# Sixteen graphs on one core: the last graph's head sums added in the bank, its last head finished apart, the check in steps, three casts on VectorE

## The chip, the cores and the metric

The kernel runs on one core of a Trainium2 chip. The metric is the device time of one execution, in microseconds (us); less is better. The engines are TensorE (PE; its loads of weights are shown on a row of their own, PEld), VectorE (DVE), ScalarE (ACT), GpSimd (POOL) and SyncE (SP), which issues the transfers here. Each engine runs its own instructions in order and waits for the others by semaphores.

## The reference, cut to what matters

Sixteen graphs of 1024 nodes with 256 features. Two layers, each followed by a layer norm over a residual sum:

```python
# layer 0: gated sum over neighbours; adj is 0 or 1 in these inputs, symmetric, with ones on the diagonal
e = leaky(einsum('bid,bjd->bij', h * a[:, 0], h))      # leaky: slope 0.2
alpha = sigmoid(where(adj == 1, e, -max))              # kinds 2 to 4 likewise with a1 to a3
x = layernorm(x + einsum('bij,bjd->bid', alpha, h) + bias)
# layer 1: graph attention, 4 heads of 64 features
Wh = (X @ W).reshape(B, N, H, F)
e = leaky_relu(e_src[:, :, None, :] + e_dst[:, None, :, :], 0.2)
alpha = softmax(where(A > 0, e, -1e9), axis=2)
x = layernorm(x + elu(einsum('bijh,bjhf->bihf', alpha, Wh)))
```

The kernel doesn't form the softmax of layer 1 edge by edge. exp(leaky_relu(s + d)) is one product of an exponential of s and one of d where s + d is positive, and another such product where it is negative. So for each head it sums two sets of columns over the neighbours j: 64 features times one factor and 64 times the other, with the two factors themselves (2 x 64 + 2 = 130 columns, called E) over the *positive* edges, and the second set (66 columns, F1) over *all* edges; the negative edges are the difference.

## The kernel before, in words

A graph has NB = 8 blocks of P = 128 nodes, in NH = 2 halves of 4 blocks (NQ = 4); a half has two pairs of blocks. `stages()` makes, for each graph, some fifty generators, one for each stage; a step of a stage issues one or a few instructions. `issue()` sorts all steps of all graphs by due times and issues them in that order: a table of times for each stage, FIRST for graph 0, TIMES for graphs 1 to 14, LAST for graph 15, with 112 added per graph. These times only order the instructions on each engine; when they run is set by the queues and semaphores. In the body, one graph's layer 0 overlaps the layer 1 of the graph before. All this stands in a block where the order is taken as written. What touches the change, with line numbers:

**The adjacency.** A block of it, 128x1024 int32, is loaded into one of two buffers (a32; aload), cast to bf16 on ScalarE (a16, one buffer; L273), with the sum of each row taken on the way (`sums`), turned (L283 on TensorE for graph 0, into a PSUM bank; L288 by a transposing DMA for the others), and written as a mask of bytes mT by ScalarE (L295, with the row sums of the squares). The two row sums are compared at the end.

**Layer 0.** The scores e (L344), leaky relu (L356 ACT, L364 DVE), sigmoid (L370 ACT), transpositions of the gate (L383 PE) and its products with the mask (L389 and L400 DVE, L407), the aggregation agg (L415 PE, 128x128 by 128x256), the residual, and the norm's parts: statistics (L432 and L438 DVE), rstd (L456 and L457, GpSimd), shift (L465 DVE), norm (L477 ACT, L475 DVE for some).

**Layer 1.** yT and the projection (L486 to L517), the two factors for each head (`product` L602 or L607), and gm, the matrix that the sums multiply. gm is held as two fp32r parts, a high one (L621 ACT) and the rest (L628 DVE), side by side: for each head and block of j, 130 high columns and then 130 low ones. `pos` (L646 DVE) writes the positive edges of a head and a half, 128x512 for each block j, into one of six buffers, from the sources broadcast by a DMA (sbc, L636 SP). The sums over the positive edges are `acc` (L658 PE): for each half and head, 8 blocks j by 4 blocks of targets q, lhsT a 128x128 piece of pos, rhs the 260 columns of gm (high and low at once), accumulated over j into a PSUM bank for each q; two PSUM tiles of two banks hold a head, and there are two such tiles (ps_u), so a head must be read out of them before the next head's sums begin. Each head is read out by a copy of its low part by ScalarE (L673) and an addition of high and low by VectorE (L681) into the tile u. The sums over all edges, tot (L701 PE), use the mask as fp32r (allm, L693 ACT) and 264 columns of gm, the high and the low part by two matmuls into the same columns: 

```python
for l in range(2):
    nc.tensor.matmul(tot[:, 0 : H * F1], lhsT=t["allm", ib, jb // 4 * 4][:, jb % 4, :],
        rhs=pl.gm[:, :, jb, l, F:E], ...
```

**The end of a graph.** For a pair of blocks and all four heads at once: total_kept or total_less (L728 ACT, L734 DVE), `weigh` (L746 ACT for the last two graphs, L758 DVE else: the second set, total less positive, times rho), `divide` (L768 to L773: sum of the sets, the softmax's denominator, its reciprocal rz, the product), `elu` (L793 ACT), `join` (L785 and L787 DVE), then the norm's parts again and `leave` (L802 SP, the store; L804 DVE, a running maximum of rz over the graphs, zinv).

**The check.** After the ordered block (L1316 to L1337) VectorE and TensorE work out whether the shortcuts held: the difference of the row sums (each entry 0 or 1), the span of the exponents, and the greatest rz, reduced and compared, transposed to one partition and reduced to a flag. `values_load` (L1339) brings the flag to the engines, and a branch (L1342) does all graphs again in a general way if it is set. With these inputs it isn't taken.

Of the kernel before, what the change touches and what calls it, by code (L numbers as in the profile page):

```python
# [8 lines left out]
F32 = mybir.dt.float32  # L9
# [160 lines left out]

class FastPools:
# [25 lines left out]
def stages(nc, k, pl, b, xg, adjg, outg, sums, span, zinv):  # L197
# [71 lines left out]
    def cast():  # L269
        for ib in range(NB):  # L270
            t["a16", ib] = pl.adjp.tile([P, N], BF16, tag="a16", name="a16", bufs=1)
            at = b * NB + ib
            nc.scalar.activation(  # L273
                t["a16", ib], t["a32", ib], AF.Copy, accum_out=sums[:, 0, at : at + 1]
            )
            yield
# [374 lines left out]

    def acc():
        for half, h in HEADS:
            for pair in range(NQ // 2):
                t["acc", half, h, pair] = pl.ps_u.tile([P, 2, HALF], F32, tag="u", name="acc")
            for jb in range(NB):
                for q in range(NQ):
                    nc.tensor.matmul(  # L658
                        t["acc", half, h, q // 2][:, q % 2, 0 : 2 * E],
                        lhsT=t["pos", half, h, jb][:, q * P : (q + 1) * P],  # L660
                        rhs=pl.gm[:, h, jb].rearrange("p l f -> p (l f)"),
                        start=(jb == 0),
                        stop=(jb == NB - 1),
                    )
                yield

    def acc_low():
        for half, h in HEADS:
            for pair in range(NQ // 2):
                low = t["low", half, h, pair] = pl.work.tile(  # L670
                    [P, 2, E], F32, tag="low", name="low", bufs=2
                )
                nc.scalar.copy(low, t["acc", half, h, pair][:, :, E : 2 * E])  # L673
                yield

    def acc_sum():
        for half, h in HEADS:
            for pair in range(NQ // 2):
                if h == 0:
                    t["u", half, pair] = pl.us.tile([P, 2, H, E], F32, tag="us", name="u")  # L680
                nc.vector.tensor_tensor(  # L681
                    t["u", half, pair][:, :, h, :],
                    t["acc", half, h, pair][:, :, 0:E],
                    t["low", half, h, pair], ALU.add,
                )
                yield
# [27 lines left out]
    def parts(half, pair):  # L714

        u = t["u", half, pair]
        return u[..., 0:F], u[..., F : 2 * F], u[..., 2 * F], u[..., 2 * F + 1]

    def second(half, pair):

        return t["u", half, pair][..., F : 2 * F + 1]

# [18 lines left out]
    def times(val, by):  # L741

        if late:
            for q in range(2):
                for h in range(H):
# [7 lines left out]
    def weigh():  # L753
        for half, pair in PAIRS:
            ib = half * NQ + 2 * pair
            u2 = second(half, pair)
            if half:
                nc.vector.tensor_tensor(u2, t["ts", pair][..., 0 : F + 1], u2, ALU.subtract)  # L758
                yield
            times(u2, t["rho"][:, ib : ib + 2])  # L760
            yield

    def divide():
        t["rz"] = small("rzs", NB, H)
        for half, pair in PAIRS:
            ib = half * NQ + 2 * pair
            o, u2, z2, z1 = parts(half, pair)
            nc.vector.tensor_tensor(o, o, u2, ALU.add)  # L768
            yield
            rz = t["rz"][:, ib : ib + 2]  # L770
# [8 lines left out]
    def join():  # L779
        for half, pair in PAIRS:  # L780
            o, ex, _, _ = parts(half, pair)
            yp = t["y", half][:, 2 * pair : 2 * pair + 2, :].rearrange(
                "p q (h f) -> p q h f", h=H
            )
            nc.vector.scalar_tensor_tensor(o, o, 0.0, yp, ALU.max, ALU.add)  # L785
            yield
            nc.vector.scalar_tensor_tensor(yp, ex, 1.0, o, ALU.min, ALU.add)  # L787
            yield

    def elu():  # L790
        for half, pair in PAIRS:
            o, ex, _, _ = parts(half, pair)
            nc.scalar.activation(ex, o, AF.Exp)  # L793
            yield

    def leave():
        for half in range(NH):
# [5 lines left out]
            if half == NH - 1:  # L803
                nc.vector.tensor_tensor(zinv, zinv, t["rz"], ALU.max)  # L804
            yield

# [11 lines left out]
        weigh=weigh(), divide=divide(), elu=elu(), join=join(),  # L818
        moments1=moments("1"), gathered1=gathered("1"),
        spread1=spread("1"), shift1=shift("1"), norm1=norm("1"), leave=leave(),  # L820
    )

# [104 lines left out]
    "leave": [206.44, 240.93],  # L927
}
FIRST = {
    "aload": [-145.70, -145.40, -144.40, -143.60, -141.20, -140.10],  # L930
    "cast": [-146.10, -145.60, -144.60, -143.90, -142.60, -142.00, -140.90, -139.50],
    "turn": [-145.90, -145.10, -144.50, -143.20, -142.30, -141.30, -140.30, -139.30],
    "mask": [-145.30, -144.90, -143.80, -142.80, -141.70, -141.10, -139.40, -139.10],
    "setup": [-142.90, -140.70, -138.30],
    "xt": [-147.20, -147.10, -147.00, -146.80],
    "xtc": [-146.90, -146.70, -146.60, -146.40],
    "xta": [-146.50, -145.80, -144.20, -142.20, -141.80, -139.90, -139.60, -137.00],
    "score": [
        -146.20, -145.50, -144.80, -144.70, -143.40, -143.10, -142.10, -141.50, -140.40,
        -138.90, -138.60, -136.60,  # L940
    ],
    "leak": [
        -145.20, -144.30, -144.10, -144.00, -143.00, -142.70, -141.60, -141.40, -139.70,
        -138.50, -137.70, -136.40,
    ],
    "leaky": [
        -145.00, -143.70, -143.50, -143.30, -142.40, -141.90, -141.00, -140.60, -139.20,
        -137.90, -137.30, -135.60,
    ],
    "sigmoid": [-142.50, -140.80, -138.20, -137.10, -136.10, -135.00, -133.50, -132.80],  # L950
    "below": [
        -140.50, -140.20, -138.80, -138.00, -137.50, -136.80, -135.70, -135.20, -134.30,
        -132.70,
    ],
    "lower": [
        -140.00, -139.80, -138.40, -136.70, -136.00, -135.90, -134.90, -134.70, -133.40,
        -131.90,
    ],
    "upper": [-139.00, -137.60, -136.50, -135.10, -134.20, -133.00, -132.30, -131.80],
    "self_loop": [-138.70, -137.40, -135.50, -134.60, -133.80, -132.50, -131.60, -131.20],  # L960
    "agg": [
        -138.10, -137.80, -137.20, -136.20, -135.30, -134.80, -134.50, -133.90, -133.60,
        -133.20, -132.60, -132.40, -132.10, -131.40, -131.30, -130.60,
    ],
    "residual": [-136.90, -134.40, -133.70, -133.30, -133.10, -132.00, -130.90, -130.20],
    "moments0": [-135.80, -134.10, -132.90, -132.20, -131.10, -130.70, -130.40, -130.10],
    "gathered0": [-135.40, -134.00, -131.70, -131.50, -130.50, -130.30, -96.07, 17.17],
    "spread0": [-131.00, 20.28],
    "shift0": [-130.80, 24.26],
    "norm0": [6.67, 11.00, 11.41, 12.51, 25.36, 25.99, 26.71, 27.01],  # L970
    "yt": [17.15, 19.47, 29.04, 29.13],
    "ytc": [19.36, 19.69, 29.17, 29.53],
    "project": [20.27, 22.38, 25.24, 26.22, 32.78, 40.85, 41.12, 41.80],
    "wh": [25.15, 27.94, 28.22, 36.80, 41.06, 42.84, 42.85, 44.25],
    "sources": [43.57, 44.67],
    "rows": [44.50, 47.17],
    "keep_rows": [46.30, 54.62],
    "top_dve": [46.04, 47.34, 49.10, 49.48, 50.03],
    "top_pe": [46.11, 49.26],
    "exps": [51.13],  # L980
    "product": [51.24, 51.61, 51.65, 55.99, 64.09, 71.97, 73.66, 74.28],
    "high": [54.44, 56.34, 58.73, 61.00, 69.95, 72.79, 74.04, 74.66],
    "low": [54.68, 57.50, 65.30, 66.50, 71.75, 77.68, 77.72, 77.72],
    "sload": [50.22, 76.32, 79.88, 84.60, 99.79, 115.99, 126.87, 141.84],
    "pos": [
        56.38, 56.65, 59.61, 60.83, 61.90, 62.47, 66.98, 72.25, 78.79, 79.58, 80.30,
        81.29, 81.91, 83.89, 85.64, 86.24, 94.25, 94.83, 97.97, 99.15, 100.99, 101.36,
        101.95, 101.97, 105.63, 106.23, 106.73, 107.47, 108.82, 109.31, 109.42, 109.44,
        111.05, 111.90, 112.37, 114.78, 114.79, 114.81, 115.82, 117.22, 117.23, 120.53,
        122.14, 122.30, 123.00, 123.69, 124.94, 127.40, 128.22, 130.84, 132.75, 133.15,  # L990
        134.26, 137.15, 140.15, 141.06, 143.44, 144.05, 145.63, 146.94, 153.65, 154.27,
        155.46, 159.89,
    ],
    "acc": [
        61.10, 61.65, 61.72, 63.59, 69.81, 72.90, 74.47, 75.10, 81.40, 83.30, 83.92,
        84.50, 84.62, 86.15, 88.72, 89.34, 98.53, 98.69, 100.90, 100.97, 102.11, 102.79,
        105.80, 106.18, 108.03, 108.18, 108.25, 109.02, 109.72, 109.72, 110.35, 110.44,
        113.56, 114.38, 116.31, 117.04, 117.43, 119.10, 119.20, 119.89, 122.26, 122.73,
        122.79, 124.03, 124.41, 124.82, 125.15, 127.73, 134.85, 139.77, 140.29, 142.76,
        143.64, 145.00, 145.14, 146.56, 153.78, 155.85, 158.96, 159.35, 164.01, 166.21,  # L1000
        166.25, 166.99,
    ],
    "acc_low": [
        76.14, 76.54, 89.55, 94.31, 106.18, 107.05, 110.80, 113.01, 119.96, 120.50,
        133.26, 133.40, 149.44, 150.74, 167.23, 167.69,
# [382 lines left out]
```

## Time and profile before

| | us |
|---|---|
| median of 3 runs | 1748.97 (1747.94 to 1749.34) |
| the profiled execution's own time | 1748.92 |
| its span, first to last instruction | 1747.1 |
| PE (TensorE) busy | 1695.6 (97%), mean granted clock 0.990 |
| DVE (VectorE) busy | 1639.0 (94%) |
| ACT (ScalarE) busy | 1237.6 (71%) |
| POOL (GpSimd) busy | 107.1 (6%) |
| acc: 4096 matmuls 128x260, L658 | 613.3, 293 ns for one |
| u<-acc,low: 256 additions, L681 | 102.1, 419 ns for one |
| low<-acc: 256 copies, L673 | 89.9, 377 ns for one |
| a<-a: 128 casts, L273 | 135.6, 1060 ns for one |

Busy time is the sum of an engine's instructions, as a share of the span. The duration of a matmul is not its cost: matmuls are pipelined, and the distance from one to the next is shorter than either. "Idle before" is the time for which an engine stood still just ahead of a group's instructions, with the event that ended it. The granted clock is the TensorE clock as a share of full speed. A row of a timeline is a run of like instructions: its start, its length, engine, line, operation, tiles, shape and number, and in brackets the wait ahead of it.

### The profile page before, as it was taken

The numbers are of one execution on the slowest core, as the hardware profiler recorded it, in microseconds if no ns is written. First come the engines' busy times: TensorE is split into PE (matmuls) and PEld (weight loads), VectorE is DVE, ScalarE is ACT, GpSimd is POOL, SyncE is SP. The second block draws the span as 40 slices with busy tenths as digits, with TensorE's granted clock in tenths as the row PEclk, the third lists the DMA queues.
The fourth block names the chain that finished last, engine by engine and source line by source line (L and its number), as shares of the span: only waits on it lengthen the run. The fifth ranks groups of instructions, "written<-read, shape, count | busy, mean of one in ns | idle before, by whom it ended". The sixth has DMA issues, their size and how long they took to land.

```text
span 1747.1 us, 29629 instructions
## 1 busy us (share of the span) xinstructions
PE 1695.6 (97%) x10579; PEld 1494.8 (86%) x10579; DVE 1639.0 (94%) x3640; ACT 1237.6 (71%) x2770; POOL 107.1 (6%) x138
## 2 busy tenths in 40 slices
PE   7999999999999999999999999999999999999884
PEld 4789898998979889898998989889898998979883
DVE  4498999999999999999999999999999999999997
ACT  6673967759587685967759586685957769585675
POOL 0001000010000101000010000101000010000100
PEclk9999999999999999999999999999999999999987
DMA  5452343434334343343434334343342435331020
GB/s 184 109 127 75 93 109 88 109 91 129 90 90 101 109 119 91 98 98 91 109 93 135 81 98 108 99 115 91 97 110 78 109 74 139 79 74 49 26 67 26
DMA packets 249274, 168.60 MB, mean 97 GB/s; under 512 B 133280, under 2 KB 232736, under 8 KB 249120
## 3 DMA queue, kind: packets, MB, share of 16 engines
q1 hardware_dynamic: 249120, 166.63, 36.3%
q8 instruction: 86, 1.41, 0.3%
q14 instruction: 68, 0.56, 0.1%
HBM read 118.10 MB, written 17.04 MB: 77 GB/s over the span
## 4 chain that ended last, share of the span: by engine, by line
PE 83%; issue 7%; DVE 4%; ACT 3%; DMA 1%; POOL 0%; SPq 0%; POOLq 0%; ACTq 0%; DVEq 0%
PE agg L415 24%; PE acc L658 24%; PE tot L701 13%; PE e L344 11%; PE pw L505 6%; PE pg L383 2%; DVE pos L646 1%; PE pt L308 1%; PE pt L486 1%; DMA sbc<-sdram 1%; DMA aT<-a 0%; ACT mT L295 0%; ACT a L273 0%; DVE gm L628 0%; DVE gate L364 0%
## 5 line engine op out<-in xcount | busy, mean ns | idle before, releaser
L646 DVE SCALAR_TENSOR_TENSOR pos<-sbc,nd,mT 128x512 fp32r<-128x512 f32 x1024 | 732.0, 738 | 7.6 <-DMA sbc<-sdram 4.5
L658 PE MATMUL acc<-gm,pos 128*128 128x260 f32 x4096 | 613.3, 293 | 6.5 <-DVE u L681 2.8
L658 PEld LDWEIGHTS acc<-gm,pos 128*128 128x128 f32 x4096 | 538.7, 190 | 19.5 <-issue 3.8
L415 PE MATMUL agg<-xb,gate 128*128 128x256 f32 x2048 | 463.3, 379 | 0.0
L415 PEld LDWEIGHTS agg<-xb,gate 128*128 128x128 f32 x2048 | 380.0, 190 | 46.9 <-DVE gate L407 0.6
L701 PE MATMUL tot<-gm,allm 128*128 128x264 f32 x2048 | 328.4, 297 | 7.1 <-ACT gm L621 5.0
L701 PEld LDWEIGHTS tot<-gm,allm 128*128 128x128 f32 x2048 | 281.1, 190 | 11.7 <-ACT gm L621 5.2
L344 PE MATMUL e<-xT,xTa 128*128 128x512 f32 (+3 forms) x768 | 265.6, 490 | 3.1 <-ACT xTa L332 1.6
L344 PEld LDWEIGHTS e<-xT,xTa 128*128 128x128 f32 x768 | 135.3, 191 | 106.9 <-issue 53.4
L673 ACT COPY low<-acc 128x260 f32<-128x260 f32 x256 | 89.9, 377 | 190.3 <-PE acc L658 190.3
L693 ACT CAST allm<-mT 128x512 fp32r<-128x512 uint8 x256 | 157.5, 616 | 27.9 <-PE tot L701 26.6
L477 ACT ACTIVATE y<-y,shift,rstd 128x256 f32<-128x256 f32 x254 | 136.8, 591 | 41.8 <-DVE shift L465 41.8
L273 ACT ACTIVATE a<-a 128x1024 bf16<-128x1024 int32 x128 | 135.6, 1060 | 41.0 <-DMA aT<-a 19.3
L295 ACT ACTIVATE mT<-aT 128x1024 uint8<-128x1024 bf16 x120 | 127.2, 1060 | 6.4 <-DMA aT<-a 6.3
L456 POOL TENSOR_SCALAR std<-mv 128x4 f32<-128x4 f32 x64 | 27.0, 421 | 1626.0 <-DVE mv L438 1426.5
L364 DVE TENSOR_TENSOR gate<-e,gate 128x512 f32<-128x512 f32 x192 | 104.2, 550 | 21.3 <-ACT gate L356 21.2
L505 PE MATMUL pw<-w_aug,yT 128*128 128x264 f32 x512 | 122.2, 387 | 0.7 <-ACT yT L495 0.6
L681 DVE TENSOR_TENSOR u<-acc,low 128x260 f32<-128x260 f32 x256 | 102.1, 419 | 16.6 <-ACT low L673 16.6
L432 DVE BATCH_NORM_STATS2 st<-y 128x6 f32<-128x256 f32 x256 | 105.8, 415 | 1.2
L505 PEld LDWEIGHTS pw<-w_aug,yT 128*128 128x128 f32 x512 | 93.4, 190 | 15.6 <-ACT yT L495 1.7
L356 ACT ACTIVATE gate<-e 128x512 f32<-128x512 f32 x192 | 90.0, 486 | 14.6 <-PE e L344 14.5
L400 DVE TENSOR_TENSOR gate<-gate,mT 128x1024 f32<-128x1024 f32 (+7 forms) x128 | 95.8, 748 | 4.5 <-PE pg L383 2.4
(97 smaller groups left out, 1775.9 us busy)
## 6 DMA issues: line engine op xcount, KB each, us to landing
a<-in_adj_dram SPq DMA_DIRECT2D x128, 512.0 KB, 4.7
sbc<-sdram SPq DMA_DIRECT2D x128, 256.0 KB, 4.6
out_dram<-y SPq DMA_DIRECT2D x31, 512.0 KB, 3.5
xb<-in_x_dram SPq DMA_DIRECT2D x15, 1024.0 KB, 5.2
aT<-a SPq DMA_TRANSPOSE x120, 3.1
xb<-in_x_dram SPq DMA_DIRECT2D x2, 512.0 KB, 4.2
sdram<-srow SPq DMA_DIRECT2D x32, 8.0 KB, 1.4
out_dram<-y SPq DMA_DIRECT2D x2, 256.0 KB, 2.3
```

What stands on the lines that cost most here:

```text
L273: nc.scalar.activation(t["a16", ib], t["a32", ib], AF.Copy, accum_out=sums[:, 0, at : at + 1])
L295: nc.scalar.activation(t["mT"][:, :, ib * P : (ib + 1) * P], t["aT", ib], AF.Square, accum_out=sums[:, 1, at : at + 1],)
L344: nc.tensor.matmul(e[:, 0:n], lhsT=t["xTa", jb][:, c, :], rhs=t["xT"][:, c, at : at + n], start=(c == 0), stop=(c == DC - 1),)
L364: nc.vector.tensor_tensor(ge, t["e", jb, at][:, 0:n], ge, ALU.max)
L415: nc.tensor.matmul(agg[:, 0:D], lhsT=t["gate"][:, jb, ib * P : (ib + 1) * P], rhs=t["xb"][:, jb, :], start=(jb == 0), stop=(jb == NB - 1),)
L432: nc.vector.bn_stats(st, t["y", half][:, q, :])
L477: nc.scalar.activation(y, y, AF.Identity, bias=shift, scale=rstd)
L505: nc.tensor.matmul(pw[:, 0:WD], lhsT=t["yT"][:, c, jb * P : (jb + 1) * P], rhs=k.w_aug[:, c, :], start=(c == 0), stop=(c == DC - 1),)
L646: nc.vector.scalar_tensor_tensor(p_, t["sbc", half, h], t["nd"][:, jb, h : h + 1], t["mT"][:, jb, half * HALF : (half + 1) * HALF], ALU.is ...
L658: nc.tensor.matmul(t["acc", half, h, q // 2][:, q % 2, 0 : 2 * E], lhsT=t["pos", half, h, jb][:, q * P : (q + 1) * P], rhs=pl.gm[:, h, jb] ...
L693: nc.scalar.copy(m_, t["mT"][:, j0 : j0 + 4, ib * P : (ib + 1) * P])
L701: nc.tensor.matmul(tot[:, 0 : H * F1], lhsT=t["allm", ib, jb // 4 * 4][:, jb % 4, :], rhs=pl.gm[:, :, jb, l, F:E], start=(jb == 0 and l == 0),
```

## The change

It has five parts.

1. In the last graph (`whole`), an acc step issues two matmuls of 130 columns, high and low, with the same lhsT and into the same columns, in place of one of 260. `acc_low` then copies the bank to u by ScalarE, and `acc_sum` does nothing.
2. The last half's last head of the last graph (`apart`) isn't copied: `weigh`, `divide`, `elu` and `join` leave it out there (`heads`), and four new stages finish it by itself, reading the bank: `weigh_end`, `divide_end`, `elu_end`, `join_end`. Joins of that half are done for each block by itself.
3. The check becomes a stage, `verdict`, of seven steps in the ordered block; its fourth step, the maximum into zinv, is done for every graph and leaves `leave`.
4. Casts 1, 3 and 5 of graph 0 are done by VectorE, a copy and a reduction each, in place of one instruction of ScalarE.
5. FIRST and LAST have new times in all rows. TIMES keeps its rows and gets times for the new stages.

```diff
+CASTS_DVE = (1, 3, 5)
...
+            if first and ib in CASTS_DVE:
+                nc.vector.tensor_copy(t["a16", ib], t["a32", ib])
+                nc.vector.tensor_reduce(total, t["a16", ib], AX.X, ALU.add)
+            else:
+                nc.scalar.activation(t["a16", ib], t["a32", ib], AF.Copy, accum_out=total)
...
+    whole = last
+    def apart(half, h):
+        return last and half and h == H - 1
...
+                    out = t["acc", half, h, q // 2][:, q % 2]
+                    lhsT = t["pos", half, h, jb][:, q * P : (q + 1) * P]
+                    if whole:
+                        for l in range(2):
+                            nc.tensor.matmul(
+                                out[:, 0:E],
+                                lhsT=lhsT,
+                                rhs=pl.gm[:, h, jb, l],
+                                start=(jb == 0 and l == 0),
+                                stop=(jb == NB - 1 and l == 1),
+                            )
...
     def acc_low():
...
+                if not whole:
...
+                elif not apart(half, h):
+                    nc.scalar.copy(t["u", half, pair][:, :, h, :], t["acc", half, h, pair][:, :, 0:E])
...
+    def heads(half):
+        return slice(0, H - 1 if last and half else H)
...
+            yp = nodes(half, pair)[:, :, heads(half)]
+            rows = (0, 1) if last and half else (slice(0, 2),)
+            for q in rows:
+                nc.vector.scalar_tensor_tensor(o[:, q], o[:, q], 0.0, yp[:, q], ALU.max, ALU.add)
...
+    def weigh_end():
+        for h, pair in END:
+            if last:
+                u2 = second(1, pair)[:, :, h]
+                acc = t["acc", 1, h, pair][:, :, F : 2 * F + 1]
+                nc.vector.tensor_tensor(u2, t["ts", pair][:, :, h, 0 : F + 1], acc, ALU.subtract)
+            yield
...
+    def divide_end():
...
+            nc.vector.tensor_tensor(z2, z2, rho, ALU.mult)
+            for q in range(2):
+                nc.vector.scalar_tensor_tensor(
+                    o[:, q], u2[:, q], rho[:, q : q + 1], acc[:, q, 0:F], ALU.mult, ALU.add
+                )
+            yield
+            z1 = acc[:, :, 2 * F + 1]
+            nc.vector.scalar_tensor_tensor(rz, z1, Z_MIN, z2, ALU.max, ALU.add)
+            yield
+            nc.vector.reciprocal(rz, rz)
+            yield
+            for q in range(2):
+                nc.vector.tensor_scalar(o[:, q], o[:, q], rz[:, q : q + 1], None, ALU.mult)
+            yield
...
+    def verdict():
+        if last:
...
+            nc.vector.tensor_reduce(more, sums, AX.X, ALU.add)
...
+        yield
...
+        nc.vector.tensor_tensor(zinv, zinv, t["rz"], ALU.max)
+        yield
...
+        if last:
+            pm = bank("pm")
+            nc.tensor.transpose(pm[0:1, 0:P], bad[:, 3:4], k.ident)
+        yield
+        if last:
+            nc.vector.tensor_reduce(good, pm[0:1, 0:P], AX.X, ALU.min)
+            nc.vector.tensor_scalar(k.flag, good, 0.0, None, ALU.is_equal)
+        yield
...
 FIRST = {
-    "aload": [-145.70, -145.40, -144.40, -143.60, -141.20, -140.10],
-    "cast": [-146.10, -145.60, -144.60, -143.90, -142.60, -142.00, -140.90, -139.50],
-    "turn": [-145.90, -145.10, -144.50, -143.20, -142.30, -141.30, -140.30, -139.30],
-    "setup": [-142.90, -140.70, -138.30],
+    "aload": [-145.70, -144.80, -142.70, -142.00, -141.30, -140.80],
+    "cast": [-145.90, -145.40, -144.30, -143.40, -142.40, -141.50, -140.30, -139.80],
+    "turn": [-145.80, -145.10, -144.00, -142.90, -141.80, -141.10, -140.10, -139.10],
+    "setup": [-144.60, -140.20, -137.20],
...
 LAST = {
-    "xload": [-123.18],
+    "xload": [-181.01],
...
+    "weigh_end": [6742.82, 6772.43],
+    "divide_end": [6879.53, 6888.09, 6902.23, 6919.73, 6950.05, 6986.68, 7018.84, 7061.32],
+    "elu_end": [6945.09, 7067.26],
+    "join_end": [7015.36, 7048.45, 7104.80, 7162.49],
+    "verdict": [7086.56, 7119.58, 7163.33, 7169.88, 7194.61, 7207.71, 7515.59],
...
-        bad = pl.small.tile([P, 4], F32, tag="bad", name="bad", bufs=1)
...
-        nc.vector.tensor_scalar(flag, good, 0.0, None, ALU.is_equal)
```

## The prediction

> **What bounds the kernel now.** I read the page first, then busy time by windows over the last 100 us, then the timeline of TensorE and of VectorE there, and last the weight loads by shape.
>
> The page's busy time, with the share of the span:
>
> ```profile
> PE 1695.6 (97%) x10579; PEld 1494.8 (86%) x10579; DVE 1639.0 (94%) x3640; ACT 1237.6 (71%) x2770; POOL 107.1 (6%) x138
> ```
>
> TensorE is the bound of the body: of the page's 40 slices it is full in all but the first and the last three, and there nothing but less TensorE work saves time. The body's order is the same before and after, so the change can act in the first 40 us and in the last graph only. Busy time by windows there (columns: length, PE, weight loads, DVE, ACT, POOL, granted clock, DMA share, GB/s):
>
> ```profile
> 1658.00:1674.00 16.00, 8.69 (x41) 8.01 (x42) 15.93 (x31) 15.97 (x58) 0.00 (x0) 0.71 0.27 82
> 1674.00:1711.00 37.00, 36.25 (x283) 35.83 (x282) 35.23 (x70) 22.03 (x62) 1.27 (x2) 0.96 0.16 44
> 1711.00:1725.00 14.00, 11.04 (x64) 9.72 (x64) 12.12 (x26) 6.07 (x23) 0.00 (x0) 0.88 0.00 1
> 1725.00:1740.00 15.00, 0.00 (x0) 0.00 (x0) 12.17 (x36) 12.36 (x42) 2.86 (x4) 0.60 0.10 35
> ```
>
> The reader is to see that the last graph's sums over neighbours (acc, tot) run from 1658.7 to 1724.6, that in the middle 37 us TensorE and VectorE are both full, so that neither has room for the other's work, and that after 1725 TensorE has no more to do: VectorE finishes heads, joins and norms. TensorE's timeline gives the pace of its two kinds of matmul:
>
> ```profile
> 1679.55 5.26 PE L701 MATMUL tot<-gm,allm 128*128 128x264 f32 x40
> 1684.66 0.64 PE L658 MATMUL acc<-gm,pos 128*128 128x260 f32 x4
> ...
> 1698.85 3.08 PE L658 MATMUL acc<-gm,pos 128*128 128x260 f32 x24
> 1701.77 0.66 PE L701 MATMUL tot<-gm,allm 128*128 128x264 f32 x4
> ...
> 1712.42 0.51 PE L658 MATMUL acc<-gm,pos 128*128 128x260 f32 x2 [1.59 <-DVE u L681]
> 1713.36 5.39 PE L658 MATMUL acc<-gm,pos 128*128 128x260 f32 x30 [0.43 <-DVE u L681]
> 1719.49 5.14 PE L658 MATMUL acc<-gm,pos 128*128 128x260 f32 x32 [0.75 <-DVE u L681]
> ```
>
> Start to start, 24 acc matmuls of 260 columns take 2.92 us, 0.122 each (the 32 of the last line: 0.120), and 40 tot of 264 take 5.11, 0.128 each. The tot loop uses one lhsT for two matmuls in a row (l = 0, 1), and still the page counts as many loads as matmuls: a repeated lhsT is loaded again.
>
> **What a matmul of 130 columns costs.** This is the step that decides, and no row shows it. The change turns the 256 acc matmuls of the last graph into 512 of half the columns, each with its own load. The weight loads by shape:
>
> ```profile
> L658 PEld LDWEIGHTS acc<-gm,pos 128*128 128x128 f32 x4096 | 538.7, 190 | 19.5 <-issue 3.8 <-DVE u L681 3.4 <-DVE pos L646 1.9
> ...
> L283 PEld LDWEIGHTS <-a 128*128 128x128 bf16 x64 | 4.5, 104 | 6.4 <-ACT a L273 3.9 <-issue 2.4
> ...
> L576 PEld LDWEIGHTS ptop<-ident,top 128*4 128x4 f32 x16 | 1.3, 81 | 0.5 <-ACT srow L540 0.3 <-issue 0.2
> ```
>
> A load of 4 columns takes 81 ns, one of a pos block, 128 columns, 190: the columns are 109 ns of it. If loads follow each other at that pace, a pos block costs about 109 ns however short the matmul behind it. The nearest warm row with such a load and a short matmul, the e piece of 128 columns:
>
> ```profile
> 1560.82 0.53 PEld L344 LDWEIGHTS e<-xT,xTa 128*128 128x128 f32 x4
> ```
>
> Four loads of 190 in 0.53 us: (530 - 190) / 3 = 113 ns apart; its matmuls' records (mean 276, four in 0.61) give 111. The two pbc matmuls of 4 columns (0.38 us together, mean 258) stand 0.12 to 0.13 apart. The near bounds are 0.109 (190 - 81) and 0.13 (pbc); the far ends are 0.060 (half of 0.120, if only streaming counted) and 0.222 (if this type lost its pace at few columns and took the two f32 passes of the e piece, 2 x 0.111). I take 0.111, of the e row, which has the same load.
>
> The page "TensorE: Matmul & The Clock Gate" of the Trainium skill, section "Back-to-back issue gap", speaks against this: it gives about 81 ns for a sustained pair of load and matmul at 128 columns. By it the sum below would have 448 x 0.081 = 36.3 us in place of 49.7, and the forecast would be 1745.7. Its section "Weight-path perf modes" says why it need not hold here: the fast weight load is left off for FP32; the rows agree as far as the load of bf16 takes 104 ns and that of pos 190.
>
> **The change, part by part.**
>
> 1. acc in two narrow matmuls. Head 0 (64 matmuls) starts at 1657.9: gm's low[1] now stands ahead of pos[2] on VectorE, 0.8 earlier than the 1658.7 of before. TensorE is cold there (granted 0.71): before, 28 matmuls took 5.4 us in place of 3.4. With 20 at 0.22 and 44 at 0.111 it ends at 1667.2, but pos[7] stands behind some 14 other VectorE steps of 0.66 on the mean (9.2) and comes at about 1667.5 with the gaps between them; then ScalarE evacuates both banks behind high[6], so head 1 starts at about 1669.5. From there the path is TensorE's alone: 56 steps x 8 = 448 matmuls x 0.111 = 49.7; tot 128 x 0.128 = 16.4; the waits for the banks before heads 6 and 7, which have little or no tot work between (two copies of 0.35 and 0.27 after the last matmul) 1.3. End: 1669.5 + 67.4 = **1736.9, against 1724.6: +12.3**.
>
> 2. The 16 adds u<-acc,low leave VectorE: 15 of them lie in 1658 to 1725, 0.34 start to start, 5.1 us, and the three waits of acc for them (1.59, 0.43, 0.75) shrink to those for the copies. ScalarE keeps 14 copies (0.37 each) and loses two. With TensorE full this pays nothing on the path: pos has six buffers, VectorE runs into them and waits. What is late next is TensorE.
>
> 3. The last head from the bank. On VectorE's queue the first step on the bank (weigh_end) stands ahead of join[2], of all of divide[8] to [15] for the other three heads, and of both joins of half 1; these wait behind it for the last matmul, as in the kernel before. I add what VectorE does from the last matmul to the last statistics, by the spacing of its rows: subtractions from the bank 2 x 0.2 (128x130; L681 at 260 takes 0.42, L407 at 128 0.28); adds 2 x 0.47; the end's products, sums and scalings of 64 columns 2 x 1.2; reciprocals and small ones 0.8; joins 2 x 0.6, 8 x 0.27 (rows apart) and 4 x 0.2; statistics 7 x 0.34; aggregates 8 x 0.1; the check's steps 1.5. Sum 13.1, against 13.0 before (1724.6 to 1737.64). Then POOL and shift, 1.5, and the norms, 0.8: again 15.4 in all. ScalarE's scalings (6 x 0.25 for a pair) and exps lie beside it. **0**, bounds -3 and +2.
>
> 4. The check in steps. Before, the zinv maximum, three reductions and comparisons, the transposition and the flag stood behind the last norm:
>
> ```profile
> 1739.30 0.73 DVE L475 TENSOR_SCALAR y<-y,rstd,shift 128x256 f32<-128x256 f32 x2
> ...
> 1741.52 0.14 DVE L1337 TENSOR_SCALAR flag<-good 1x1 int32<-1x1 f32 x1
> ```
>
> From 1740.03 to 1741.66 they are alone: **-1.6**. The last stands now beside POOL's rstd, ahead of shift. The 5.4 us after it (each engine loads the flag, branches, drains) stay. Bounds -1.6 and 0, if the branch waits for the last store instead.
>
> 5. Start: three casts on VectorE. ScalarE loses 3 x 1.25 (1.06 and the read of the sum, 0.19). VectorE gains three copies (about 1.2, as L400's 128x1024) and three sums (0.40 for 256, so 1.2 to 1.4): 7.6 us, where it is busy 8.5 of 30 us. But casts take turns over one bf16 block and two int32 blocks: cast, transposition, next cast, and a load of 4.7 us after the cast before the last. Followed through, cast[3] stays at 20.2, turn[3] goes from 22.1 to 22.9 (it stands behind score[5] now), and mask[7], which frees upper[0] and the aggregation, ends at 36.7 against 36.5. SP issues setup's three loads ahead of two adjacency loads, which wait for casts anyway. What is gained is two gate transpositions done before the aggregation (0.44 each): **-0.5**, bounds -5.8 (all of TensorE's 10.2 idle us before 38.5 but the first 4.4) and +1.5.
>
> 6. The last graph's loads, casts and turns move among graph 13's and 14's steps, its x load and two turns past graph 13's sloads on SP. From 1372 to 1640 TensorE is idle for 1.4 us in all by its windows, and its work there is the same: **0**, bounds -2 and +2.
>
> Sum: +12.3 + 0 - 1.6 - 0.5 = +10.2. The profiled execution has a span of 1747.1 and a time of 1748.92, 1.8 around it, which is the median of the runs (1748.97) as near as matters. 1747.1 + 10.2 + 1.8 = **1759.1 us**. With 0.109 and half of the good bounds of 3, 5 and 6: -0.9 -1.5 -2.7 -1 = 1753. With 0.13 it is 448 x 0.019 = 8.5 more, and with the bad bound of 3 1770.
>
> **Rivals.**
>
> Not slower, **the load is hidden**: 130 columns cost half of 260. TensorE would end at 1669.5 + 27 + 17.7 = 1714, VectorE decides, 5.1 earlier than before: 1719.5. With 4 and 5: 1741.7. It ends level with before at 0.088 us a matmul ((1726.7 - 1669.5 - 17.7) / 448). For it: the gaps of acc behind u. Against: the rows above, all over 0.1. This is also the case that a load is skipped for a repeated lhsT, against tot's loads. 9%.
>
> **The gain elsewhere pays it back**: 0.109, the start's and the order's whole bounds and half of the tail's: -0.9 -5.3 -2 -1.5 = 1749.4, no change that can be told. For it: ScalarE is busy 9.97 of the 10 us from 20 to 30. Against: the chain of part 5. 11%.
>
> **Narrow matmuls lose their pace**: 0.222, by the type or because a half-filled array is granted half the clock (the granted clock falls to 0.71 where TensorE is half busy). 448 x 0.111 more and 5 in head 0: 1814. No row shows either. 10%.
>
> **How the numbers follow.** The forecast, 1753 to 1770, holds 70%. Repeated measurement of this kernel tells about 0.2%, 3.5 us, from no change. Of the hidden load 8 of 9 are faster, the pay-back is the same zone, 1 in it comes from the hidden load: faster 0.08, same 0.12, slower 0.80. The range goes from 1745 to 1774: the forecast, the pay-back and a little above for the unknown pace, and leaves the other two out.
>
> **What would show it.** Part 1: the last graph's acc, now 512 of 128x130, 0.111 apart; below 0.088 the forecast is wrong in sign. Part 2: VectorE's pos waits for acc between 1680 and 1735. Part 3: last matmul to last norm 15.4. Part 4: flag ahead of the last norm. Part 5: the first aggregation at 38. The forecast is wrong if a load is skipped for a repeated lhsT, or if the start moves by more than 3 us.

## The result, and the profile after

The changed kernel takes 1765.37 us (median of 6 runs, 1763.71 to 1767.4) where the kernel before takes 1749.32 beside it (6 runs, 1747.94 to 1753.23): slower, ratio 1.0089, 95% interval 1.0076 to 1.0102. The forecast was 1759.1, 10.2 more; it came to 16.0 more, inside the range of 1745 to 1774. The profiled execution took 1763.71 us, with a span of 1761.9: 14.8 more than the span before. Marks and timelines below count in spans; the result of each experiment is a time.

Page of the changed kernel, busy time:

```profile
PE 1722.9 (98%) x10835; PEld 1526.2 (87%) x10835; DVE 1642.6 (93%) x3654; ACT 1234.0 (70%) x2756; POOL 105.7 (6%) x138
```

256 more matmuls, and 27.3 us more of TensorE. Windows over the last graph (length, PE, weight loads, DVE, ACT, POOL, granted clock, DMA share, GB/s):

```profile
1655.00:1669.40 14.40, 14.06 (x66) 13.88 (x66) 13.88 (x27) 12.88 (x45) 0.00 (x0) 0.50 0.25 73
1669.40:1678.30 8.90, 8.90 (x43) 8.90 (x43) 4.86 (x10) 4.73 (x18) 0.00 (x0) 0.50 0.01 2
1678.30:1725.50 47.20, 47.20 (x408) 47.20 (x408) 33.18 (x57) 22.24 (x61) 2.02 (x2) 1.00 0.14 40
1725.50:1740.20 14.70, 14.68 (x130) 14.39 (x128) 11.31 (x22) 8.29 (x32) 0.00 (x0) 1.00 0.00 1
1740.20:1761.90 21.70, 0.96 (x3) 0.58 (x3) 13.21 (x66) 7.58 (x22) 2.59 (x4) 0.57 0.16 51
```

Two things are to be seen. The load column equals the PE column; with wide matmuls it was nearly so too (35.83 of 36.25 in the middle window of before), so that each narrow matmul waits for its load is left to the experiments to show. And TensorE, without a pause, runs at half clock for 23 us. Its timeline:

```profile
1654.95 0.48 PE L676 MATMUL acc<-gm,pos 128*128 128x130 f32 x1 [3.11 <-ACT gm L628]
1655.77 6.88 PE L676 MATMUL acc<-gm,pos 128*128 128x130 f32 x31 [0.34 <-DVE gm L635]
1662.44 0.41 PE L536 MATMUL ps<-ident,src 128*16 128x128 f32 x1
1662.51 12.19 PE L676 MATMUL acc<-gm,pos 128*128 128x130 f32 x56
1674.50 1.19 PE L731 MATMUL tot<-gm,allm 128*128 128x264 f32 x4
...
1677.09 1.78 PE L731 MATMUL tot<-gm,allm 128*128 128x264 f32 x8
...
1725.55 14.65 PE L676 MATMUL acc<-gm,pos 128*128 128x130 f32 x128
```

The last 128 stand 0.112 apart (median of the spacing), those of the second and fourth line about 0.213. The wait of 3.11 us ahead of head 0 lets the clock fall. The kernel before has such waits too (2.61 and 1.74 us), and there 4.4 us of wide matmuls bring it back, at 1663.1; its window and its timeline:

```profile
1656.30:1663.10 6.80, 4.79 (x21) 4.53 (x22) 6.77 (x12) 6.77 (x26) 0.00 (x0) 0.50 0.00 0
1663.10:1669.90 6.80, 1.91 (x14) 1.49 (x12) 6.76 (x16) 6.80 (x23) 0.00 (x0) 1.00 0.34 108
```

```profile
1658.69 5.57 PE L658 MATMUL acc<-gm,pos 128*128 128x260 f32 x28 [1.74 <-DVE gm L628]
```

In the changed kernel it comes back only at 1678.3, in the midst of the second run of wide tot matmuls.

Where the 14.8 us come from, by marks in both traces. The transposition of the last graph's maximum of scores (ptop) comes at 1648.18 in place of 1650.29: -2.1. From there to the last matmul's end 92.0 in place of 74.3: +17.7. From there to the end of VectorE's last norm 14.6 in place of 15.4: -0.8. From that norm to the end 7.1 in place of 7.0: +0.1.

### The profile page after: what moved, and what is told of

Read it like the earlier page. It is cut to its first block, busy times and chain, and to the rows that moved or that the text cites. A ratio compares the mean times of both kernels' runs of the same rounds, so it can differ in the third digit from the quotient of the medians.

```text
span 1761.9 us, 30150 instructions
## 1 busy us (share of the span) xinstructions
PE 1722.9 (98%) x10835; PEld 1526.2 (87%) x10835; DVE 1642.6 (93%) x3654; ACT 1234.0 (70%) x2756; POOL 105.7 (6%) x138
## 5 line engine op out<-in xcount | busy, mean ns | idle before, releaser
L684 PE MATMUL acc<-gm,pos 128*128 128x260 f32 x3840 | 570.1, 292 | 0.1
L684 PEld LDWEIGHTS acc<-gm,pos 128*128 128x128 f32 x3840 | 500.6, 189 | 10.3 <-issue 1.2
L702 ACT COPY low<-acc 128x260 f32<-128x260 f32 x240 | 84.5, 377 | 185.5 <-PE acc L684 184.7
L711 DVE TENSOR_TENSOR u<-acc,low 128x260 f32<-128x260 f32 x240 | 96.3, 421 | 8.8 <-ACT low L702 8.7
L407 DVE TENSOR_TENSOR gate<-gate,mT 128x1024 f32<-128x1024 f32 (+7 forms) x128 | 96.1, 751 | 5.6 <-PE pg L390 3.1
L363 ACT ACTIVATE gate<-e 128x512 f32<-128x512 f32 x192 | 90.1, 485 | 10.4 <-PE e L351 10.2
```

The costliest lines, as they stand in the source:

```text
L684: nc.tensor.matmul(out[:, 0 : 2 * E], lhsT=lhsT, rhs=pl.gm[:, h, jb].rearrange("p l f -> p (l f)"), start=(jb == 0), stop=(jb == NB - 1),)
```

## The experiments

The theory: the pace of the loads (0.112 a matmul, whatever its columns) and a half clock that narrow matmuls can't lift make the loss. The rivals: the loss lies in the other parts; the pace alone makes it; the columns set the pace.

**All but parts 1 and 2.** The changed kernel with

```diff
-    whole = last
+    whole = False
...
```

and with no head finished apart; the additions are issued again just behind their copies.

> The changed kernel, but the last graph's acc is one matmul of 260 columns again, with its copy and its addition, and its last head isn't finished apart; the casts on VectorE, the check in steps and the new order stay. Theory (the narrow matmuls cost it: their pace, and the half clock in which they hold TensorE after the wait ahead of the last graph's acc): the changed kernel has at 1648 a lead of 2.1 us over the kernel before, the rest goes as before, so 1747 us (1744 to 1751), the kernel before being at 1749.3. Rival (the new order, the last head or the check cost it): it stays above 1757.

1751.78 us (12 runs; ratio 1.0012, 1.0002 to 1.0021). Parts 3 to 5 make at most 4 of the 16 us of loss (by the interval); but the 1747 of the theory failed as well. From ptop to the end it takes 101.3 us where the kernel before takes 96.8: in an order made for a VectorE without additions, these come late, and acc waits for them (2.64, 1.04, 0.93, 1.49 and 2.37 us ahead of heads).

**Part 1 alone**, on the kernel before:

```diff
+                    if last:
+                        for l in range(2):
+                            nc.tensor.matmul(
+                                t["acc", half, h, q // 2][:, q % 2, 0:E],
+                                lhsT=t["pos", half, h, jb][:, q * P : (q + 1) * P],
+                                rhs=pl.gm[:, h, jb, l],
+                                start=(jb == 0 and l == 0),
+                                stop=(jb == NB - 1 and l == 1),
+                            )
+                        continue
...
```

with the copy to u by ScalarE and no addition.

> The kernel before with part 1 alone: in the last graph's acc two matmuls of 130 columns, ScalarE copies the sum, VectorE adds nothing. Theory (pace 0.112 and half clock): 1749.3 + 16 = 1765 us (1761 to 1770), with TensorE at half clock for over 15 us from the first narrow matmul on. Rival A (the pace alone costs, the clock comes back after some 4 us as in the kernel before): 1749.3 + 12 = 1761, clock back by 1665. Rival B (the cost is elsewhere in the change): under 1755.

1778.49 us, ratio 1.0163 (1.0148 to 1.0177): 29 us more, nearly double the change, and well above the theory's 1761 to 1770. Windows:

```profile
1658.00:1676.00 18.00, 13.58 (x63) 13.39 (x63) 13.24 (x26) 12.88 (x45) 0.00 (x0) 0.52 0.17 51
1676.00:1696.00 20.00, 19.85 (x90) 19.55 (x91) 10.16 (x23) 8.68 (x31) 0.00 (x0) 0.50 0.08 21
1696.00:1753.50 57.50, 56.90 (x490) 56.25 (x488) 37.98 (x61) 22.64 (x65) 2.02 (x2) 1.00 0.10 29
```

The clock stays down for 38 us and comes back within the long row of tot, which stands later in this order (1692.9). Rival A, with the clock back by 1665, is out. About 1 of the 29 us lies outside the span (3.1 us of the time do here, 2.0 in the kernel before).

**Head 1 wide.** The changed kernel with

```diff
-    whole = last
+    def whole(half, h):
+        return last and (half, h) != (0, 1)
...
```

> The changed kernel, but head 1 of half 0 of the last graph uses 32 matmuls of 260 columns, with copies and additions, in place of 64 of 130. Theory (narrow matmuls don't bring the clock back, wide ones do in some 4.3 us): the granted clock comes back about 4.3 us after head 1's first matmul (1669.4), at 1673.7 in place of 1678.4, and the time is 6.6 us less: 1759 (1757 to 1762). Rival (the clock comes back by time, or by the tot matmuls alone): back at 1678 again, and only the smaller number of loads in head 1 counts: 2 to 3 us less, 1763.

1765.35 us (1759.01 to 1767.66; ratio to the kernel before 1.0084, 1.0063 to 1.0106): the median is no better than the change, and the expected 1757 to 1762 failed. The clock did what the theory says, and then more:

```profile
1655.00:1669.00 14.00, 13.63 (x65) 13.52 (x65) 13.48 (x26) 12.58 (x44) 0.00 (x0) 0.50 0.25 75
1669.00:1672.00 3.00, 3.00 (x15) 2.77 (x15) 1.86 (x4) 2.67 (x10) 0.00 (x0) 0.53 0.02 5
1672.00:1682.50 10.50, 9.37 (x74) 8.95 (x72) 9.86 (x24) 9.10 (x28) 1.49 (x2) 1.00 0.09 26
1684.00:1698.00 14.00, 14.00 (x73) 14.00 (x73) 6.82 (x10) 3.17 (x9) 0.00 (x0) 0.55 0.34 95
```

Three us of wide matmuls bring the clock back. Then head 2 waits 1.10 and 0.44 us for the additions that the wide head needs, the clock falls, and narrow matmuls hold it at a half for 14 us again. One of the four executions did take 1759.01 us, with a mean granted clock of 0.988 where the other three had 0.983 to 0.984; that the clock wasn't lost a second time there is likely, but no trace shows it.

**260 columns twice.** The same loads, the columns doubled:

```diff
-                                out[:, 0:E], lhsT=lhsT, rhs=pl.gm[:, h, jb, l],
+                            n = 2 * E if jb < NB - 1 else E
+                            row = pl.gm[:, h].rearrange("p j l f -> p (j l f)")
+                            at = (2 * jb + l) * E
+                                out[:, 0:n], lhsT=lhsT, rhs=row[:, at : at + n],
...
```

> The changed kernel, but in 7 of 8 blocks each of the two matmuls of the last graph's acc has 260 columns in place of 130: the second 130 go into columns of the bank that nobody reads. Same loads, twice the columns. Theory (the load sets the pace, and the streamed columns set the clock): 0.120 apart in place of 0.112, +3.6 us for 448, and the half clock ends some 4 us after it began, before head 1: -4.5; the sum about -1: 1764 us (1761 to 1768). Rival (the streamed columns set the pace): 448 times 0.06 to 0.11 more, 1790 to 1815.

1760.79 us, just under the expected 1761 to 1768, ratio 1.0062 (1.0048 to 1.0077): with twice the columns it is *faster* than the change (1.0089, 1.0076 to 1.0102). Windows and the last 128 matmuls:

```profile
1658.00:1662.00 4.00, 4.00 (x24) 4.00 (x24) 4.00 (x8) 4.00 (x16) 0.00 (x0) 0.63 0.00 0
1662.00:1739.90 77.90, 75.60 (x619) 74.96 (x618) 58.05 (x106) 42.88 (x135) 2.02 (x2) 1.00 0.14 38
```

```profile
1724.21 15.65 PE L679 MATMUL acc<-gm,pos 128*128 128x260 f32 x128
```

15.65 us where 130 columns took 14.65: doubling the columns (in 7 of 8 blocks) costs 0.008 a matmul, and the clock is full 4.6 us after the first matmul (1657.8 to 1662.4) and stays so. That the columns set the pace is out, and so is that the loads hold the clock down: there are as many here.

**Wide start, then narrow.** As the last, with n = 2E in heads 0 and 1 of half 0 only.

> The changed kernel, with the last graph's acc matmuls of heads 0 and 1 of half 0 at 260 columns each as in the run with 260 columns throughout (the second 130 into columns that nobody reads), and the other six heads at 130 as in the change. Theory (narrow matmuls don't raise the clock from a half, but keep a full one): half clock for about 4 us from 1657 on, then full to the last matmul; 0.112 apart in the six heads, so 384 times 0.008 = 3 us less than the 1760.8 of the run with 260 throughout: 1758 us (1755 to 1761). Rival (narrow matmuls lose a full clock as well, so the columns had to stay wide): half clock again from head 2 on, 1765 or more.

1761.25 us, ratio 1.006 (1.0045 to 1.0075): not the 3 us better that were expected, and not told from the run before; but the narrow heads lose no clock. It is full from 1674 to the last matmul, with six narrow heads 0.112 apart. Narrow matmuls keep a full clock. Where the 3 us went is shown in part: from ptop to the end the profiled execution takes 109.9 where that of the run before takes 111.2, though it lost its clock once more around the start of head 1 (1670 to 1674, granted 0.60), behind a wait of 1.90 us. By an estimate that cost up to 1.7 (half of the 3.4 us at half clock). With the clock nearly kept up, then, the ratio falls from 1.0089 to 1.006: some 11 of the 16 us stay, the loads' pace above all, and some 5 are the half clock's.

**66 columns.** As the last, and in the other six heads:

```diff
+                            c0 = F if l and (half or h > 1) else 0
...
+                                out[:, c0:n], lhsT=lhsT, rhs=row[:, at + c0 : at + n],
...
```

> The run before (heads 0 and 1 at 260 columns), and in the other six heads the second matmul of each pair has only the last 66 of the 130 columns: the low part of the first 64 is left out of the sums there. Same loads, a quarter fewer columns in those heads. Theory (the load sets the pace): 0.11 apart as before, so the time of the run before within 2 us. Rival (the columns set the pace below 260): 192 times 0.055 = 10 us less.

1767.46 us, ratio 1.0105 (1.0089 to 1.012): a quarter fewer columns, 6 us *slower*, where the theory had it level within 2. The spacing alternates, 0.080 and 0.145, in sum 0.225 a pair as before: the load sets the pace here too. And now a full clock is lost:

```profile
1661.00:1720.60 59.60, 58.17 (x493) 57.81 (x492) 46.09 (x83) 33.99 (x103) 2.02 (x2) 1.00 0.19 50
1720.60:1728.00 7.40, 7.40 (x61) 7.40 (x60) 6.95 (x14) 1.95 (x9) 0.00 (x0) 0.88 0.00 0
1728.00:1743.00 15.00, 14.88 (x70) 14.74 (x70) 4.58 (x10) 6.29 (x23) 0.00 (x0) 0.50 0.01 1
```

Between 1661 and 1720 wide tot matmuls stand among the narrow ones and the clock holds; in the last two heads none do, and with loads back to back it falls at 1726.3, 5.6 us after the first of them.

**The start alone**, the casts and FIRST on the kernel before:

> The kernel before with part 4 and the new order of graph 0 alone: three casts on VectorE. Theory: the first aggregation starts some 0.5 us earlier or later (37.5 to 40.5, by the state of the clock in the first 13 us), TensorE waits from 27 to 34 in place of 20 to 34 in pieces and falls to half clock there, and graph 1 begins as before: 1749 to 1750 us, no change. Rival (ScalarE bound the start): 5 us less, 1744.

1750.58 us, ratio 1.0004 (0.9995 to 1.0013): no change, as the theory said. That ScalarE bound the start is out. **The last graph's order alone**, the rows of LAST from xload to exps:

> The kernel before with the new due times of the last graph for its loads, casts, turns and layer 0 alone (up to the exponentials); sums and end as before. Theory: this order brings the last graph's maximum of the scores (ptop, 1650.3 in the kernel before) forward by 2.8 us, as between graph 13 and that point in the changed kernel, and most of it stays: 1747 us (1745.5 to 1748.5). Rival (the gain is lost again, since VectorE and ScalarE then bound head 0): 1749.3.

1748.58 us, ratio 0.9995 (0.9986 to 1.0004). In its trace the last graph gains 2.7 us on graph 13 (against the kernel before, ptop goes from +1.08 to -1.65), but the measured time isn't told from no change. The trace of the kernel before flatters the gain: from ptop of graph 13 to that of graph 15 it takes 211.4 us, the other four traces of the old order 210.0 to 210.8, the eight of the new one 208.6 to 208.7. And part of the gain is lost outside the span: 2.8 to 3.6 us of the time lie there in all eleven executions, 1.9 to 2.2 in the kernel before, so that the median span is 1745.5 against 1746.8. Why stays open. **The check alone:**

> The kernel before with part 3 alone: the check in steps, its flag set ahead of the last shift. Theory (SyncE's load of the flag stands behind the last two stores on its queue, so the branch there waits for the last norm and not for the check): from the last norm to the end 6.6 to 7.0 us, where the kernel before has 7.07: 1749 us, 0 to 0.5 us less. Rival (the check stood alone on the path): 1.6 us less, 1747.4.

1749.38 us, ratio 1.0003 (0.9994 to 1.0012). From VectorE's last norm to the end it takes 6.0 in place of 7.0, more of a gain than expected; and it loses more ahead of the norm, 17.2 from the last matmul in place of 15.4. VectorE's timeline:

```profile
1737.17 0.41 DVE L810 TENSOR_REDUCE more<-sums 128x2 f32<-128x256 f32 x1
1737.62 0.16 DVE L811 TENSOR_TENSOR more<-more 128x1 f32<-128x1 f32 x1
1737.69 0.19 DVE L812 TENSOR_SCALAR span<-span 128x64 f32<-128x64 f32 x1
1737.92 0.29 DVE L813 TENSOR_REDUCE worst<-span 128x1 f32<-128x128 f32 x1
...
1740.62 0.14 DVE L845 TENSOR_SCALAR flag<-good 1x1 int32<-1x1 f32 x1
```

These stand between the joins and the statistics that all wait for. In the kernel before their matmul (pmore) ran at 1705, beside acc: the check's first half was hidden already.

**Idle matmuls.** If the clock matters, the kernel before should gain where it waits:

```diff
+    def fill():
+        for n in (18, 6, 4):
+            warm = bank("warm")
+            for _ in range(n):
+                nc.tensor.matmul(warm[:, 0:WD], lhsT=k.ones, rhs=k.w_aug[:, 0, :], start=True, stop=True)
+            yield
...
```

> The kernel before, with 28 idle f32 matmuls of 264 columns in the last graph (18 ahead of its first tot, 6 ahead of head 6 and 4 ahead of head 7 of its acc, which nobody reads), where TensorE waits for gm and for the banks. Theory (the clock falls to a half in those waits, and the acc behind them runs 4 us at half pace each time): the granted clock stays at 1.0 from 1672 to 1676 and from 1713 to 1718, worth up to 2 us each, less what VectorE then bounds: 1746.5 us (1745 to 1748.5). Rival (VectorE, full from 1674 to 1711, bounds these stretches): the clock stays up and the time is 1749, or more where the idle matmuls stand in the way.

The windows of the kernel before (first two) and of this run (next two):

```profile
1672.00:1676.00 4.00, 3.79 (x17) 3.79 (x18) 3.47 (x9) 3.81 (x15) 0.00 (x0) 0.50 0.18 52
1712.00:1718.00 6.00, 5.15 (x28) 4.94 (x29) 5.64 (x11) 1.88 (x8) 0.00 (x0) 0.72 0.01 3
```

```profile
1664.00:1674.00 10.00, 9.63 (x49) 8.46 (x50) 9.68 (x21) 9.91 (x34) 0.00 (x0) 1.00 0.45 133
1710.00:1718.00 8.00, 8.00 (x55) 7.48 (x54) 7.97 (x15) 3.86 (x13) 0.00 (x0) 1.00 0.00 0
```

The clock stays up, and the time is 1748.92 us, ratio 0.9997 (0.9988 to 1.0006): from ptop to the end 96.1 in place of 96.8. The rival holds: with 260 columns, VectorE bounds these stretches, and in this order a half clock is nearly free. **Both together**, that order and 14, 6 and 4 of the idle matmuls:

> The kernel before with the two edits that were each half a microsecond to the good and not to be told from it: the new order of the last graph's layer 0, and idle matmuls (14, 6 and 4 pairs of passes) in the last graph's waits. Theory (the order brings the last graph forward by 2.6 us in its traces, and the clock kept up saves 0.7 to 1 behind it): 1746.5 us (1745 to 1748), a little faster than both kernels. Rival (head 0 is bound by VectorE and ScalarE, which take the lead back): 1749.

1744.17 us, ratio 0.9967 (0.9954 to 0.998): faster than the kernel before and the change. Its ptop is 0.47 us ahead of the kernel before, and from there to the end it takes 93.8 in place of 96.8; where head 1 began at half clock in the kernel before, it now runs through:

```profile
1665.26 6.39 PE L715 MATMUL warm<-w_aug,ones_r 128*128 128x264 f32 x28
1671.30 1.59 PE L701 MATMUL tot<-gm,allm 128*128 128x264 f32 x8
1672.72 3.52 PE L658 MATMUL acc<-gm,pos 128*128 128x260 f32 x28
```

The medians of the two alone were 0.5 and 0.1 us better, these together are 4.9; their intervals reach to 2.4 and 2.1, so a plain sum is not far off, and whether they help each other stays open. The single traces speak for it: from ptop to the end the order alone takes 96.8 and the idle matmuls alone 96.1, both together 93.8. (An f32 matmul shows as two, so 28 are 14.)

## Why the prediction was right, and where it was short

**Part 1, the pace: right.** 0.111 was taken from the e row, 0.112 measured, and the reason held: twice or three quarters of the columns leave the load's pace as it is, within 0.008. The page "TensorE: Matmul & The Clock Gate" of the Trainium skill, section "Back-to-back issue gap", with its 81 ns, does not hold for this load of 128 f32 columns.

**Part 1, the clock: the term that was mis-sized.** "With 20 at 0.22 and 44 at 0.111 it ends at 1667.2" took it for granted that the clock comes back after some 4 us of matmuls, as in the kernel before. It didn't: all 64 of head 0 ran at 0.21 to 0.22. The start of head 1 was still as forecast (1669.4 against 1669.5), but only because the new order had brought the last graph forward by 2.1; that was luck. Then 8.9 us of head 1 ran at half clock, worth 4.4 by an estimate (half of them). The waits for the banks took 1.0 less than put in, and the pace 0.4 more; -0.4 is left over. So from head 1 to the last matmul 70.8 against 67.4 us, and the step from ptop +17.7 against +12.3. The rival "half the clock" was priced as if all 512 ran so (1814); some 100 did. The forecast held the two apart, where the truth is one inside the other.

The same page, section "What's actually happening", lets the clock come up after about 3.4 us of sustained activity. The wide matmuls agree as far as they need some 3 to 5 us. The narrow ones don't: here they run for 18.7 us at half clock ahead of the first wide tot (1655.8 to 1674.5), and in the run with part 1 alone for 13.6 and 12.0 us.

**Part 2: right.** VectorE waits for acc by way of pos, as forecast; the pages of before and after have

```profile
L646 DVE SCALAR_TENSOR_TENSOR pos<-sbc,nd,mT 128x512 fp32r<-128x512 f32 x1024 | 732.0, 738 | 7.6 <-DMA sbc<-sdram 4.5
L653 DVE SCALAR_TENSOR_TENSOR pos<-sbc,nd,mT 128x512 fp32r<-128x512 f32 x1024 | 735.0, 741 | 19.8 <-PE acc L676 8.6
```

8.6 us of it are for the last graph's acc; before, acc made 2.8 in all. So the 16 additions taken off VectorE paid nothing that shows; no run takes them off alone.

**Part 3: right within its bounds**, -0.8 against 0. The listed terms add up to 13.4, not to the 13.1 given; from the last matmul to the last statistics it took 12.2 (13.0 before). After the last matmul's end VectorE is hardly ever idle:

```profile
1739.79 0.29 DVE L845 TENSOR_TENSOR u<-ts,acc 128x130 f32<-128x130 f32 x1 [2.87 <-PE acc L676]
1740.00 0.17 DVE L445 BATCH_NORM_AGGREGATE mv<-st 128x2 f32<-128x6 f32 x1
1740.24 0.29 DVE L845 TENSOR_TENSOR u<-ts,acc 128x130 f32<-128x130 f32 x1
...
1746.84 0.39 DVE L906 TENSOR_REDUCE more<-sums 128x2 f32<-128x256 f32 x1
...
1752.58 0.14 DVE L941 TENSOR_SCALAR flag<-good 1x1 int32<-1x1 f32 x1
1753.85 0.16 DVE L472 SCALAR_TENSOR_TENSOR shift<-mv,rstd 128x4 f32<-128x4 f32 x1 [1.13 <-POOL rstd L464]
```

**Part 4: wrong**, -1.6 against +0.1 here; its other bound came true. "They are alone" overlooked ScalarE's last norm (to 1740.39) and the issue of the last store (to 1740.82), which ran beside these steps, and what the check's first half had been hidden behind. The flag is now set 1.3 us ahead of the last shift, but SyncE loads it only behind its last store (issued 1755.2, the load at 1756.6) and branches 2.0 us after ScalarE's last norm (2.1 before). TensorE's branch does end earlier, 2.5 us after that norm in place of 5.6, but its DRAIN, one of the last instructions of each engine, comes only at 1761.2, 1.5 us behind SyncE's. Of seven traces with the check in steps, three (all but parts 1 and 2, head 1 wide, the check alone) have TensorE's DRAIN first and take 5.5 to 6.0 us from VectorE's last norm to the end; the other four take 6.8 to 7.3, the six with the old check 6.9 to 7.6. Why TensorE's DRAIN comes early or late stays open.

**Part 5: right in size by chance.** The first aggregation starts at 38.00 against 38.49, the -0.5 of the forecast. But this execution had its clock up for the first four scores (1.96 us; 3.75 in the kernel before). With slow scores the old start is ahead: ptop of graph 0 at 79.7 to 79.9 in four traces, 80.4 to 81.5 in three of the new start. With fast scores the two overlap: 77.8 and 79.9 with the old start, 79.0 to 80.6 in four traces of the new one. By graph 13 the changed kernel is 0.7 behind. VectorE's casts took 0.69 us each, not 1.2.

**Part 6: wrong**, a gain where 0 stood, and outside the bound of 2 in this pair of traces: ptop goes from +0.7 in graph 13 to -2.1 in graph 15, a gain of 2.8 (1.4 to 2.8 by the other traces of the old order). The sum of what was measured, +17.7 - 0.8 + 0.1 + 0.7 - 2.8, is 14.9, the 14.8 but for rounding. This gain, which was not forecast, hid half of the 5.4 us by which part 1 was short: that the total came so near is in part luck.

## What to carry to other kernels

Before a matmul is split into narrower ones, set the pace of its weight load (here 109 ns estimated, 0.112 measured) beside the time of its columns: below it, only the number of loads counts. Then ask what the narrow stream does to the clock: a wait ahead of it can cost half the speed for as long as it lasts. And look where an engine's work was hidden before moving it: the check's first half cost nothing where it stood, and some 1.7 us ahead of the last norm where the run with the check alone put it.

## What was not expected of the hardware

The granted clock follows the share of time in which columns stream, it seems, not the share in which TensorE is busy. An estimate from the bf16 transpositions (128 columns, 0.056 apart, so 0.44 ns a column): 260 columns stream for 114 of 120 ns and raise the clock in some 3 to 5 us; 130 for 57 of 112 neither raise a half nor lose a full clock; 66 and 130 in turn, 43 of 112, lose it within 6 us. In all three the engine shows as fully busy. The rule behind it was not measured beyond these three points. In each of the 13 traces all changes of the granted clock lie whole multiples of 3.41 us apart (in the changed kernel 1654.45, 1678.34 and 1743.19: 7 and 19 of them), so when it changes seems to hang also on where a stretch of matmuls or a wait falls on that grid.
